# A first cross attention whose preparation is split into pieces of one step each, with every engine's order written out

## The chip, the cores and the metric

One core of one Trainium2 chip runs the whole program. The metric is the device time in microseconds (us) of one execution. Its engines are called by the profile's names: PE (TensorE matmul), PEld (its weight loads), DVE (VectorE), ACT (ScalarE), POOL (GpSimd) and SP (SyncE, which issues most DMAs).

## What is computed

The reference runs eight blocks one after the other on `x` (8 batches x 256 tokens x 128) and a context (8 x 512 x 96). The change is in the first block, a cross attention with 16 heads of 8 elements, and in the seams beside it:

```python
Qp = query @ Wq + bq                      # query = layernorm(x)
K = _l2norm(key @ Wk + bk)                # key = value = the context
V = value @ Wv + bv
Q = _l2norm(Qp)
scores = jnp.einsum('bhqd,bhkd->bhqk', Q, K) * SCALE     # 16 heads of 8
attn = jax.nn.softmax(scores, axis=-1)
out = jnp.einsum('bhqk,bhkd->bhqd', attn, V)
out = out @ Wo + bo
x = out + Qp
return (x - mu) / jnp.sqrt(var + LN_EPS) * ln_gamma + ln_beta
```

The block's result is added to `x`. The second block, a feed-forward network (FFN) with eight experts, begins with two norms of `x`, a router of 8 logits, and a choice of the top two.

## The kernel before

**Tiling.** `x` lies as 16 tiles of 128 tokens. A *group* is four of them, two batches. For every batch b the keys are prepared (context transposed, `turn_ctx`; projected and biased, `biased_k`; the rows' squares and their inverse roots, `row_sizes`; scaled, `scaled_rows`; transposed and cut into three bf16 parts, `pieces`; stored to DRAM as `kd` and read back as `kS`, eight heads of 72 rows). For every even b the queries of its group are prepared alike (`norm_x`, `turn_x`, `project_q`, `pieces`, then `qd` and `qS`). `project_v` makes the values, and `place_values` copies them on POOL into a ring of two tiles `va`, whose columns of ones make a head's sum of exponentials appear as one more row of its product.

**The loop.** A batch has 8 steps, 64 in all: a step does two of four head pairs' scores (`step_probs`: eight score matmuls `sc`, and two ACT exponentials of 128x1024, L617) and, two steps behind, the value products (`step_values`: sixteen `po` records). Four steps make a *half* of a batch, eight heads. `half_sums` then copies `po` to `pv` on ACT (L633). In the next step `half_values` multiplies `pv` by the matrix `moves`, which brings every head's sum to all of its 16 rows, takes the reciprocal of 128x256 (L641) and multiplies (L642). `finish` applies Wo (`pw`), adds the base `qpo`, norms (L654 to 656) and adds to `x_sb` on POOL (L657). `normed_group` (two norms, `z`) and `route_group` (the transposes of `z`, the router's `pl`, softmax and top two) prepare the FFN.

**The order.** `at_step(t, name, f, ...)` enters a piece into `plan`; `beside(t)` runs in step t all that is due, after the scores' matmuls and ahead of the value products. Matmuls and transposes keep the written order. Ahead of the loop all engines do (`in_order`). In the loop the other engines' order is a scheduler's choice, except that nothing in it goes ahead of what is written before the loop (`fenced`), and that pieces given through `queued` keep their own order. A piece has one step: its matmuls, its DVE and POOL operations, and its DMAs are all written there.

**Memory that turns.** `banks("l0x", 2, 2)`: two pairs of PSUM banks for scores, two banks for `po`, and two single banks which all other matmuls (`pt`, `pct`, `pk`, `pq`, `pv`, `pd`, `pw`, `pl`) take in turn (`bank`). `kS` and `qS` have three buffers each, `ct`, `un`, `cut`, `v0` two, `qp`, `kp`, `sq`, `pv0` one.

**SP** issues, in the plan's steps: a batch's context at t0-24, the loads of `kS` and `qS` at t0-8 and t0-4 (t0 = 8b), a group of `x` at 6 and 16, 15 broadcasts of biases (`load_bc`) at 10, rows of biases at 17, and FFN weights at 18, 26 and 42. `spread_rows` builds a matrix for a much later block, in six pieces on POOL at steps 21 to 31 (L160 to L169).

Of the kernel before, what the change touches and what calls it, by code (L numbers as in the profile page):

```python
# [9 lines left out]
F32 = mybir.dt.float32  # L10
# [21 lines left out]
def kernel(ctx: ExitStack, tc: tile.TileContext, a: dict, out: bass.AP):  # L32
# [50 lines left out]

    @contextmanager
    def fenced():

        traced = nc.cur_bb.bb.instructions
        last = traced[-1]
        before = {i.engine: i for i in traced}
        yield  # L90
        start = next(k for k in reversed(range(len(traced))) if traced[k] is last) + 1
        for i in traced[start:]:
            if i.engine in before:
                behind(i, before[i.engine])

    def queued(f, *args):
        with in_order():
            f(*args)
# [227 lines left out]
    def layernorm(src, dst, n):  # L326
# [7 lines left out]
        rsqrt(rstd[:, :n], mv[:, :n, 1], n, LN_EPS, ALU.add)  # L334
        for t in range(n):
            nc.vector.tensor_scalar(
                dst[:, t, :], src[:, t, :], mv[:, t, 0:1], rstd[:, t : t + 1], ALU.subtract, ALU.mult
            )

# [64 lines left out]

    def normed_group(pool, g):
# [3 lines left out]
        layernorm(x_sb[:, gs], xl[:, gs], 4)  # L409
        nc.gpsimd.tensor_tensor(x_sb[:, gs], x_sb[:, gs], xl[:, gs], ALU.add)  # L410
        layernorm(xl[:, gs], z, 4)
# [4 lines left out]
    def route_group(pool, g, z):  # L416

        gs = slice(4 * g, 4 * g + 4)
        transpose4(z, xlT[:, 512 * g : 512 * (g + 1)])
        pl = bank("pl")[:, : 4 * NE].rearrange("p (t e) -> p t e", e=NE)  # L420
# [5 lines left out]
        softmax8(pool, p, 4)  # L426
# [9 lines left out]
    with banks("l0x", 2, 2), tc.tile_pool(name="l0x", bufs=2) as pool, tc.tile_pool(  # L436
# [21 lines left out]
        def norm_x(g):  # L458
            gs = slice(4 * g, 4 * g + 4)
            layernorm(x_sb[:, gs, :], xl[:, gs, :], 4)  # L460
# [4 lines left out]
        def row_sizes(src):  # L465

            sq = pool.tile([P, 4, D], F32, tag="sq", name="sq", bufs=1)
            nc.gpsimd.tensor_tensor(sq, src, src, ALU.mult)
# [11 lines left out]
        def unit_rows(src):  # L480

            return scaled_rows(src, row_sizes(src))

        def pieces(un, name, first=False):

# [12 lines left out]
            else:  # L498
                nc.gpsimd.tensor_copy(cut[:, 1, :], rest)
                nc.gpsimd.tensor_tensor(cut[:, 2, :], rest, cut[:, 1, :], ALU.subtract)  # L500
            if name == "kd":
# [40 lines left out]

        moves = pool.tile([P, P], F32, name="moves", bufs=1)

        def make_moves():
            m, i = (v.rearrange("p (g h o) -> p g h o", g=4, h=2) for v in (moves, ident))
            for h in range(2):
                nc.gpsimd.tensor_copy(m[:, :, h], i[:, :, 1])

# [12 lines left out]
        def output_base(g, qp):  # L562

            gs = slice(4 * g, 4 * g + 4)
            nc.gpsimd.tensor_tensor(qpo[:, gs], qp, over(bc["L0_xattn_bo"], 4), ALU.add)
            nc.gpsimd.tensor_tensor(x_sb[:, gs], x_sb[:, gs], over(bc["L0_xattn_ln_beta"], 4), ALU.add)

        def project_q(g):
            qp = biased_q(g)
            un = unit_rows(qp)  # L570
            output_base(g, qp)
            return un
# [12 lines left out]
        def project_k(b):  # L585
            return unit_rows(biased_k(b))
# [44 lines left out]
        def half_sums(po):  # L631
            pv = pool.tile([P, S], F32, tag="pv0", name="pv0", bufs=1)
            nc.scalar.copy(pv, po)  # L633
            return pv

        def half_values(pv, oT, half):

            pd = bank("pd")[:, :S]
            matmul(pd, lhsT=moves, rhs=pv, start=True, stop=True)
            den = pool.tile([P, S], F32, tag="den0", name="den0")  # L640
            nc.vector.reciprocal(den, pd)  # L641
            nc.vector.tensor_tensor(oT[:, half], pv, den, ALU.mult)  # L642

        def finish(b, oT):
# [10 lines left out]
            layernorm(y, y, 2)  # L655
# [11 lines left out]
        at_step(0, ("kd", 1), pieces, ("un_k", 1), "kd")  # L667
        for b in range(B):
            t0 = 8 * b

            if b >= 2:
                late = t0 - 16 if b == 2 else t0 - 21
                at_step(t0 - 24, ("ct", b), load_ctx, b)
                if b % 2 == 0:
                    at_step(late, ("xl", b), norm_x, b // 2)
                    at_step(late + 2, ("xlT", b), turn_x, b // 2)
                at_step(late + 1, ("turn", b), turn_ctx, b, ("ct", b))
                at_step(late + 1, ("max", b), max_ctx, b)
                if b % 2 == 0:
                    at_step(late + 3, ("un_q", b), project_q, b // 2)  # L680
                at_step(late + 4, ("un_k", b), project_k, b)
                at_step(late + 5, ("v", b), project_v, b)
                if b % 2 == 0:
                    at_step(late + 6, ("qd", b // 2), pieces, ("un_q", b), "qd")
                at_step(late + 7, ("kd", b), pieces, ("un_k", b), "kd")
            for half in range(2):
                if (b, half) != (0, 0):
                    at_step(t0 - 8 + 4 * half, ("kS", b, half), stacked_k, ("kd", b), half)
                    at_step(t0 - 8 + 4 * half, ("qS", b, half), stacked_q, ("qd", b // 2), half, b % 2)
                    at_step(t0 - 2 + 4 * half, ("va", b, half), place_values, b, half, ("v", b))  # L690
            at_step(t0 + 11, ("done", b), lambda b, oT: finish(b, oT), b, ("oT", b))
        for g in range(4):
            at_step(16 * g + 20, ("z", g), normed_group, pool, g)
            at_step(16 * g + 26, ("r", g), route_group, pool, g, ("z", g))
# [3 lines left out]
        at_step(3, ("moves", 0), make_moves)  # L698
# [1201 lines left out]
```

## Time and profile before

| | us |
|---|---|
| runs | 1621.91, 1623.96, 1627.40 |
| median | 1623.96 |
| the profiled execution | 1627.38 |
| its span | 1625.7 |

| group in the loop (33.6 to 258 us) | count | busy us | mean ns |
|---|---|---|---|
| ACT `pT<-sc` 128x1024 (L617) | 128 | 124.3 | 1026 |
| PE `po<-pT,va` (L60) | 1024 | 78.7 | 430 |
| PE `sc<-qS,kS` (L60) | 508 | 77.8 | 298 |
| PE `pd<-pv,moves` (L60) | 30 | 10.2 | 423 |
| POOL `ln_rstd` and `l_inv` 128x4 (L324) | 18 | 18.4 | 1018 |
| POOL spread rows (L160 to L169) | 24 | 16.5 | 688 |
| DVE `rest<-pt,cut` (L494) | 10 | 6.7 | 672 |
| ACT `pv<-po` (L633) | 16 | 6.1 | 380 |

A float32 matmul is two records, a transpose and a bf16 matmul are one. Records of PE overlap a little, so that its busy sum is not its time; the distance between two starts is. In rows of the timeline the columns are start, length, engine, line, operation, tiles, and in brackets the idle time ahead of it with what ended it.

### The profile page before, as it was taken

Reading aid. Unit: us, or ns where it says so; the run is one execution under the profiler, and the core shown is the slowest. Engines: PE = TensorE matmul, PEld = TensorE weight load, DVE = VectorE, ACT = ScalarE, POOL = GpSimd, SP = SyncE. Lnnn points to the kernel's source line nnn. Section 1 sums busy time; section 2 is a strip of 40 time slices with the busy share of each in tenths; the row PEclk is TensorE's granted clock in tenths of the full one; section 3 lists DMA queues with packets and bytes.
Section 4 is the critical chain, followed back from the end, with each engine's and each line's share of the span. In section 5 each row is a group of like instructions: output and inputs, shape, how many; then the busy total and the mean of one; then the engine's idle time right before and its main releaser. Section 6 shows DMA issues by size and latency. Waiting matters only on the chain.

```text
span 1625.7 us, 24905 instructions
## 1 busy us (share of the span) xinstructions
PE 1518.5 (93%) x9038; PEld 900.6 (55%) x9041; DVE 1000.9 (62%) x2444; ACT 819.8 (50%) x1671; POOL 505.9 (31%) x680
## 2 busy tenths in 40 slices
PE   5898798999997898999999999999999999999996
PEld 4555455776464474565555554555555555555554
DVE  5565656786776546667764555666666665656563
ACT  2564575454755655556553222545555545455552
POOL 4456321001222223333440001324243424334342
PEclk9887899999999898999999999999999999999997
DMA  5563330020511113121200000000000000000000
GB/s 124 147 152 85 100 87 27 1 71 14 185 52 53 41 44 97 60 78 54 78 27 1 1 1 1 1 1 7 4 8 4 7 4 11 1 10 6 6 8 13
DMA packets 72519, 67.90 MB, mean 42 GB/s; under 512 B 17059, under 2 KB 61390, under 8 KB 70862
## 3 DMA queue, kind: packets, MB, share of 16 engines
q1 hardware_dynamic: 69518, 63.68, 13.5%
q0 software_dynamic: 1536, 2.11, 0.4%
q8 instruction: 72, 1.18, 0.3%
q10 hardware_dynamic: 1344, 0.52, 0.1%
q14 instruction: 49, 0.40, 0.1%
HBM read 44.80 MB, written 21.50 MB: 41 GB/s over the span
## 4 chain that ended last, share of the span: by engine, by line
PE 75%; DVE 10%; POOL 5%; ACT 5%; issue 3%; DMA 1%; POOLq 0%; SPq 0%; ACTq 0%; DVEq 0%
PE sc L60 14%; PE poh L60 11%; PE tp L63 11%; PE po L60 6%; PE ph L60 4%; PE pkh L60 3%; PE poe L60 3%; PE pqh L60 3%; PE acc L60 3%; PE pox L60 2%; PE pkv L60 2%; PE pvh L60 2%; POOL ln_rstd L324 2%; PE pyw L60 2%; PE pxv L60 2%
## 5 line engine op out<-in xcount | busy, mean ns | idle before, releaser
L1438 POOL TENSOR_SCALAR prob<-prob,at_inv 128x512 f32<-128x512 f32 x384 | 261.7, 695 | 482.9 <-DVE at_inv L1436 375.7
L1451 ACT COPY probT<-tp 128x512 f32<-128x512 f32 x192 | 112.8, 587 | 335.2 <-PE tp L63 333.9
L1431 ACT ACTIVATE prob<-sc,at_neg 128x512 f32<-128x512 f32 x384 | 261.3, 688 | 32.9 <-DVE at_neg L1428 28.4
L1428 DVE TENSOR_REDUCE at_neg<-sc 128x2 f32<-128x1024 f32 x192 | 233.3, 1216 | 65.6 <-PE sc L60 65.3
L63 PEld LDWEIGHTS tp<-ident,prob 128*128 128x128 f32 x1664 | 178.4, 141 | 147.9 <-issue 101.3
L63 PE MATMUL tp<-ident,prob 128*128 128x128 f32 x1664 | 227.1, 279 | 1.5 <-POOL prob L1438 1.4
L60 PE MATMUL sc<-kTh,qT 64*128 64x512 f32 x768 | 217.6, 644 | 0.0
L60 PE MATMUL poh<-probT,vh 128*64 128x256 f32 x1536 | 186.5, 385 | 1.8 <-ACT vh L1402 1.0
L617 ACT ACTIVATE pT<-sc 128x1024 f32<-128x1024 f32 x128 | 124.3, 1026 | 76.1 <-PE sc L60 75.5
L324 POOL TENSOR_TENSOR ln_rstd<-rs_v,mhalf 128x4 f32<-128x4 f32 (+1 forms) x52 | 48.0, 924 | 354.2 <-DVE rs_v L323 342.4
L60 PEld LDWEIGHTS poh<-probT,vh 128*64 128x64 f32 x1536 | 101.9, 136 | 78.1 <-issue 14.1
L1451 DVE COPY probT<-tp 128x512 f32<-128x512 f32 x192 | 130.5, 679 | 1.1 <-PE tp L63 0.9
L60 PEld LDWEIGHTS sc<-kTh,qT 64*128 64x128 f32 x768 | 58.4, 186 | 81.7 <-issue 51.4
L1436 DVE RECIPROCAL at_inv<-at_tot 128x2 f32<-128x2 f32 x192 | 31.6, 164 | 100.7 <-ACT prob L1431 79.5
L60 PE MATMUL sc<-qS,kS 72*128 72x256 bf16 x512 | 78.6, 299 | 4.1 <-DMA qS<-qd 3.5
L1463 DVE COPY oTh<-poh 128x256 f32<-128x256 f32 x96 | 40.7, 424 | 62.3 <-PE poh L60 60.4
L60 PE MATMUL po<-pT,va 128*32 128x256 f32 x1024 | 78.7, 430 | 0.2 <-ACT pT L617 0.2
L1431 ACT ACTIVATION_READ_ACCUMULATOR prob<-sc,at_neg 128x1 f32 x384 | 77.5, 202 | 0.0
L60 PEld LDWEIGHTS <-kS 72*128 72x128 bf16 x512 | 49.0, 106 | 44.4 <-issue 31.5
L943 ACT ACTIVATE hT<-ph,cols 128x512 f32<-128x512 f32 x64 | 43.3, 687 | 52.3 <-PE ph L60 48.9
L60 PE MATMUL pkh<-ctxT,w 96*128 96x512 f32 x128 | 67.0, 605 | 0.0
L60 PE MATMUL pvh<-w,ctxT 96*128 96x512 f32 x128 | 66.4, 600 | 0.0
(386 smaller groups left out, 2417.6 us busy)
## 6 DMA issues: line engine op xcount, KB each, us to landing
kS<-kd SPq DMA_DIRECT2D x48, 192.0 KB
kTh<-kv SPq DMA_DIRECT2D x6, 1024.0 KB
vh<-kv SPq DMA_DIRECT2D x6, 1024.0 KB
kv<-xl SPq DMA_DIRECT2D x20, 256.0 KB
qd<-cut SPq DMA_DIRECT2D x24, 192.0 KB
qS<-qd SPq DMA_DIRECT2D x48, 96.0 KB
kv<-shelf SPq DMA_DIRECT2D x16, 256.0 KB
kd<-cut SPq DMA_DIRECT2D x8, 384.0 KB
```

The costliest lines, as they stand in the source:

```text
L60: return tc.keep_in_program_order(nc.tensor.matmul(*args, **kw))
L63: return tc.keep_in_program_order(nc.tensor.transpose(*args, **kw))
L324: nc.gpsimd.tensor_tensor(dst, v[:, :n], mhalf[:, :n], ALU.pow)
L617: nc.scalar.activation(pT[:, g], sc, AF.Exp, scale=8.0 ** -0.5)
L943: nc.scalar.activation(hT[:, c, :], ph, AF.Gelu, bias=col("L0_ffn_b1", 2 * e + c))
L1428: nc.vector.tensor_reduce(neg, sc, AX.X, ALU.max, negate=True)
L1431: nc.scalar.activation(prob[:, q, h, :], sc[:, h, :], AF.Exp, bias=neg[:, one], scale=1.0, accum_out=tot[:, one])
L1436: nc.vector.reciprocal(inv, tot)
L1438: nc.gpsimd.tensor_scalar(prob[:, q, h, :], prob[:, q, h, :], inv[:, h : h + 1], 1.0, ALU.mult, ALU.mult)
L1451: copy(probT[:, h, :, q * P : (q + 1) * P], tp)
L1463: nc.vector.tensor_copy(oT[:, c, :], po)
```

## The change

- `layernorm` becomes `norm_sizes` (statistics, variance, inverse root) and `norm_rows`; `row_sizes` becomes `row_squares` and `row_inverses`; `pieces` becomes `cut_pieces` and `store_pieces`.
- Longer pieces are generators whose stages `in_stages` puts on a list of steps: queries over six steps, keys over five within six, values of a half over three, `finish` over two, `normed_group` over three, `route_group` over three.
- The whole loop now stands within `in_order`, so that every engine keeps the written order; `fenced` and `queued` go. `beside(t - 1)` runs in pass t, so a piece of plan step t stands one pass later than that number. "Pass t" below is the loop's t.
- `moves` goes. A half's sums are taken from `pv` transposed: two matmuls of `pv` with 8 columns of the identity give 32 sums for each query; their reciprocals are widened on POOL (`wide`, 128x256), transposed by two transposes (`pd`), and multiplied with `pv`.
- Loads of `kS` and `qS` stand at t0-6 and t0-2; `residual_base` is a stage of its own.
- The six `spread_rows` pieces move to the plan of the FFN stage, steps 16 to 26, which isn't within `in_order`.
- `route_group` of group 2 comes nine steps behind its `z`, after the loop's last scores.

```diff
-        def half_sums(po):
+        first_sums = ident.rearrange("p (g h j m) -> p g h j m", g=4, h=2, j=2)[:, :, 1, :, 0]
+        def half_values(po, oT, half):
             pv = pool.tile([P, S], F32, tag="pv0", name="pv0", bufs=1)
             nc.scalar.copy(pv, po)
-            return pv
-        def half_values(pv, oT, half):
+            yield
+            ps = bank("ps")[:, :16].rearrange("p (q g j) -> p q g j", q=2, g=4)
+            for q in range(2):
+                matmul(ps[:, q], lhsT=pv[:, q * P : (q + 1) * P], rhs=first_sums, start=True, stop=True)
+            inv = pool.tile([P, 2, 4, 2, 2], F32, tag="inv0", name="inv0")
+            for h in range(2):
+                nc.vector.reciprocal(inv[:, :, :, h, :], ps)
+            wide = pool.tile([P, 2, P], F32, tag="wide0", name="wide0", bufs=1)
+            nc.gpsimd.tensor_copy(
+                wide.rearrange("p q (i m) -> p (q i) m", m=8),
+                inv.rearrange("p q g h j -> p (q g h j)").unsqueeze(2).to_broadcast([P, 32, 8]),
+            )
+            yield
             pd = bank("pd")[:, :S]
-            matmul(pd, lhsT=moves, rhs=pv, start=True, stop=True)
-            den = pool.tile([P, S], F32, tag="den0", name="den0")
-            nc.vector.reciprocal(den, pd)
-            nc.vector.tensor_tensor(oT[:, half], pv, den, ALU.mult)
+            for q in range(2):
+                transpose(pd[:, q * P : (q + 1) * P], wide[:, q], ident)
+            nc.vector.tensor_tensor(oT[:, half], pv, pd, ALU.mult)
...
+        def unit_pieces(biased, name, n, base=None):
+            p = biased(n)
+            sq = row_squares(p)
+            yield
+            inv = row_inverses(sq)
+            yield
+            un = scaled_rows(p, inv)
+            yield
+            cut = cut_pieces(un)
+            yield
+            got[name, n] = store_pieces(cut, name)
+            if base:
+                output_base(n, p)
+                yield
+                residual_base(n)
...
+        def in_stages(ts, name, f, *args):
+            stages = []
+            def run():
+                if not stages:
+                    stages.append(f(*[got[v] if isinstance(v, tuple) else v for v in args]))
+                try:
+                    next(stages[0])
+                except StopIteration as end:
+                    got[name] = end.value
+            for t in ts:
+                plan.append((t, len(plan), run))
...
+            late = 0 if b == 2 else t0 - 19
             if b >= 2:
-                late = t0 - 16 if b == 2 else t0 - 21
-                at_step(t0 - 24, ("ct", b), load_ctx, b)
+                at_step(late - 1, ("ct", b), load_ctx, b)
                 if b % 2 == 0:
-                    at_step(late, ("xl", b), norm_x, b // 2)
+                    in_stages((late, late + 1), ("xl", b), norm_x, b // 2)
                     at_step(late + 2, ("xlT", b), turn_x, b // 2)
-                at_step(late + 1, ("turn", b), turn_ctx, b, ("ct", b))
+                at_step(late + 3, ("turn", b), turn_ctx, b, ("ct", b))
...
+                    in_stages(
+                        (late + 4, late + 5, late + 6, late + 7, late + 8, late + 9), ("q", b),
+                        unit_pieces, biased_q, "qd", b // 2, True,
+                    )
+                at_step(late + 4, ("max", b), max_ctx, b)
+                in_stages(
+                    (late + 5, late + 6, late + 7, late + 9, late + 10), ("k", b), unit_pieces, biased_k, "kd", b
+                )
+                at_step(late + 8, ("v", b), project_v, b)
...
+                t = t0 + 5 + 4 * half
+                in_stages((t, t + 1, t + 2), ("o", b, half), half_values, ("po", b, half), ("oT", b), half)
+            in_stages((t0 + 12, t0 + 13), ("done", b), finish, b, ("oT", b))
-        for g in range(4):
-            at_step(16 * g + 20, ("z", g), normed_group, pool, g)
-            at_step(16 * g + 26, ("r", g), route_group, pool, g, ("z", g))
+        for g in range(3):
+            t = 16 * g + 22
+            in_stages((t, t + 1, t + 2), ("z", g), normed_group, pool, g)
+            if g == 2:
+                t += 9
+            in_stages((t + 3, t + 4, t + 5), ("r", g), route_group, pool, g, ("z", g))
...
-        fence = fenced()
-        fence.__enter__()
...
+            for t in range(8 * B + 2):
...
+                if t > 0:
+                    beside(t - 1)
...
-        at_step(1, normed_group, pool, 3, to="z")
+        at_step(1, lambda: whole(normed_group(pool, 3)), to="z")
...
+        for r in range(2):
+            for i in range(3):
+                at_step(16 + 6 * r + 2 * i, spread_rows, r, i)
```

## The prediction

> **What bounds the kernel now.** I read the slices of the page first, then the windows by stage, then TensorE's order of time inside the first attention, then the groups of that stage.
>
> ```profile
> PE   5898798999997898999999999999999999999996
> ...
> PEclk9887899999999898999999999999999999999997
> ```
>
> Seen here: slices 0 to 5 (a slice is 40.6 us) are the first cross attention, and there TensorE is neither full nor at full clock. Behind slice 7 both rows stand at 9, so little is to be won there, and nothing there is edited. The windows (columns: PE, PE load, DVE, ACT, POOL busy with counts, granted clock, DMA share, GB/s) cut the attention at its stalls:
>
> ```profile
> 0.00:32.50 32.50, 14.55 (x60) 12.48 (x61) 14.98 (x31) 5.43 (x9) 13.51 (x23) 1.00 0.50 129
> 32.50:57.80 25.30, 22.45 (x153) 14.98 (x154) 12.89 (x31) 12.11 (x13) 10.23 (x13) 0.81 0.58 130
> 57.80:110.40 52.60, 50.26 (x511) 32.63 (x508) 33.09 (x78) 37.08 (x45) 26.13 (x37) 0.93 0.59 148
> 110.40:134.60 24.20, 16.89 (x133) 10.73 (x130) 13.29 (x31) 8.78 (x12) 15.92 (x21) 0.77 0.43 100
> ```
>
> Compare the counts: 511 matmul records in 52.6 us, 133 in 24.2 us. Where nothing waits, TensorE runs at a step of 2 to 2.9 us; from 110.4 on it lost over half. TensorE's order of time shows how:
>
> ```profile
> 110.35 1.05 PE L60 MATMUL sc<-qS,kS 72*128 72x256 bf16 x8
> 114.90 2.07 PE L60 MATMUL pk<-w,ctxT 96*128 96x128 f32 x8 [3.51 <-DVE ctxT L451]
> 116.91 1.94 PE L60 MATMUL po<-pT,va 128*32 128x256 f32 x16
> ...
> 127.79 0.66 PE L63 MATMUL pt<-ident,un 128*128 128x128 f32 x4 [1.87 <-DVE v L596]
> 129.54 0.63 PE L63 MATMUL pt<-ident,z 128*128 128x128 f32 x4 [1.10 <-DVE den L641]
> 130.95 1.87 PE L60 MATMUL pl<-w,xlT 128*128 128x8 f32 x8 [0.78 <-DVE xlT L108]
> 132.76 1.94 PE L60 MATMUL po<-pT,va 128*32 128x256 f32 x16
> ```
>
> A piece of preparation sits in TensorE's queue and its input is late in VectorE's; then the same sixteen value products take 1.94 us and not 1.07 (half clock). So each wait is paid twice. The bound of this stage is TensorE's in-order queue waiting on chains VectorE-GpSimd-VectorE.
>
> **The size of it.** From the first score (32.52) to the first matmul of the FFN (262.93) are 230.4 us. TensorE's own work, from full-clock starts (eight sc 0.98 us, sixteen po 1.00, eight pk, pv, pq, pw or pl 0.89, four pt or pct 0.45 to 0.55, two pd 0.45): 64 x 1.98 = 126.7; 12 pk/pv 10.7; 6 pct 3.3; 16 pt 7.2; 3 pq 2.7; 16 pd 7.2; 8 pw 7.2; 3 pl 2.7; rest 0.2. Sum 167.9, so 62.5 us are lost to waits and clock. That is the most the change can win.
>
> **Part by part.**
>
> *Inverses.* These rows are touched:
>
> ```profile
> L641 DVE RECIPROCAL den<-pd 128x256 f32<-128x256 f32 x15 | 26.3, 1756 | 26.0 <-PE pd L60 26.0
> L601 POOL COPY va<-v 128x256 f32<-128x256 f32 x14 | 5.5, 396 | 21.1 <-PE po L60 21.1
> L565 POOL TENSOR_TENSOR xl<-qp,bc_tile 128x512 f32<-128x512 f32 x3 | 3.8, 1269 | 0.0
> ```
>
> VectorE loses 16 x 1.76 and gets 16 x 2 reciprocals of 16 elements; the nearest row, the reciprocal of 128x4, is 0.18 each. Net -1.4 us a half, -22 in all, off TensorE's path except that work stops queueing behind it. TensorE: pd 0.45 becomes ps (two products, half of a pl: 0.45) and two transposes (half of a pt, 0.22, taken 0.30): +0.30 x 16 = **+4.8 us**, on the path. GpSimd gets `wide`, 128x256, with no row of its own: between 0.40 (the va copy, as many elements) and 1.27 (row L565, twice as many and two inputs); I take 0.5, nearest the copy. The handover ps, reciprocals, `wide`, transpose is 0.1+0.35+0.1+0.5+0.1 = 1.15 us against 1.98 us of po and sc that lie between on TensorE, so it is hidden with 0.8 to spare, and the pieces ahead of it on GpSimd are few in each pass.
>
> *Pieces, one a pass.* For each pass I added the pieces' rows by engine. TensorE is largest in nearly all (2.0 to 3.5 us); over 64 passes TensorE has 170, ScalarE 138, VectorE 112, GpSimd 89 us. VectorE overflows where routing falls (18 small operations of 0.22 and others: 5.4 us in passes 28 and 44), GpSimd where the norm falls (5.0 us in passes 23 and 39). Most handovers now have a pass or two in hand: q from pq to its transposes is 5.0 us of chain against three passes (8 us). The context's load for b=3 went out at 44.61 for transposes that waited for it until 49.52 (2.82 us and more); now it is issued in pass 5 for pass 9, behind few DMAs, and I take that wait as gone. The residual's beta (1.27 us of GpSimd) only changes its place, and a second sq buffer costs nothing. Four remain late:
>
> 1. *z.* Its three stages stand in passes 23, 24, 25, and TensorE's transposes of z in pass 26, ahead of that pass's value products and next scores. Taking 0 at the scores of pass 23: ScalarE's cast ends 3.3, rest 4.0, sizes 5.5; GpSimd has `wide`, va, residual and the cut's two operations first and raises the power by 7.1; rows 8.3, sizes 9.8, power 11.0, rows 12.2, gamma 12.9, GpSimd's beta 14.3 (rows 1.12, 1.53 for four statistics, 1.02, 1.27). TensorE arrives after 2.88+2.28+2.53+0.98 = 8.7. **Wait 5.7 us**, for groups 0 and 1; group 2's transposes are moved by 9 and do not wait.
> 2. *xl* in passes 16 and 32: waits of 1.0 and 1.4 by the same sum.
> 3. *After routing* (passes 28 to 31): v's bank is cleared behind it, the next transposes wait some 2 us; twice, 4.
> 4. *qS at pass 16.* SP has the kd store (pass 11), then the 15 broadcasts, in this trace from 76.15 to 85.73 = 9.6 us, then kS and qS, 2.7 us, landing within 2.7 (88.57 to the use at 91.25). The loads moved two steps later; from pass 11 they land 16.9 us on, and pass 16 starts 14.2 on. 0 to 2.7 of wait, up to 3.5 of half clock; I take 3.
>
> *The clock.* The rule of the Trainium skill (TensorE: Matmul & The Clock Gate, Part 1) is that the array falls to half rate after an idle window of about 3.4 us. By it only the z waits would cost clock. The trace is stricter: after 1.90 us idle at 144.05 the products at 145.81 took 1.94 us, and some 4.7 us were lost until 155. By the rule, the waits listed under 2 to 4 cost their 9.4 us; by the row each that nears 2 us costs up to 4.7 more. But after 1.29 us at 164.53 the next sc took 1.05, so I charge waits under 1.5 us nothing, and 1.6 us after each z wait (as after 181.55: pd 1.19, po 1.94, sc 1.20 where 0.60, 1.07, 1.05 are usual): z costs 2 x 7.3 = 14.6.
>
> *Spread rows* are moved out of this stage (16.5 us of GpSimd). The order list shows them not in the FFN but hoisted to the ramp, all six pieces ahead of or between the ramp's own GpSimd work (a piece is 0.52+1.28+0.75 or 1.16). Two go ahead of sq<-kp: GpSimd was free from 7.3 to 10.8, they take 5.5, so kp's squares start 2.0 later, and kd, qd and the first scores +2.2. The skill (SBUF — State Buffer, section on its two sides) adds that VectorE with two SBUF inputs and GpSimd lock each other out for a whole instruction; the trace agrees (un at 92.52 took 1.52, 0.69 alone, beside sq). By the rows alone +2.2, with that lock +3; **+3.0** taken, bounds 0 and 5.
>
> *End and FFN.* Last po to first ph was 5.0 us; now 0.48+0.45+0.45+1.05+0.3+0.5+0.89, about the same, 2.5 of it waiting. Group 2's routing now lies behind it on VectorE, 20 x 0.22 ahead of the last y, so group 3's norm and its pl come up to 3.7 later: 0 to 3.7, **+2.0**. TensorE's order behind it is the same in both.
>
> **Sum.** Work 167.9+4.8 = 172.7. Losses kept: cold start 4.5 (three steps at half clock, as now), coupling 6 (passes 15 to 23 took 21.98 us for 20.86 of work, 5%, in the loaded two thirds), z 14.6, xl 2.4, routing 4, qS 3, end 2.5 = 37.0. Together 209.7 against 230.4: -20.7; ramp +3.0, FFN +2.0: **-15.7 us**. The profiled run took 1627.38 (its span 1625.7 and 1.7 around it): 1611.7. The median, 1623.96, is 3.4 lower: **1608.3**.
>
> **Rivals.** *More is won (0.10):* the coupling is nil and z's waits fall in passes that are long anyway. For it: VectorE is freed of 22 us. Against: the chain of z is longer than three passes whatever they hold. -15.7-6.0-14.6 = -36.3: 1588. *It is given back (0.13):* pinning makes ScalarE and VectorE stand where the scheduler let other work pass; twice the coupling (+6), qS at its upper bound (+3), waits of 1 to 2 us at the row's clock (+6): about 1623. For it: only two single banks turn for all pieces, three of them in passes 27 and 43. Against: the loads by pass. *Slower (0.15):* `wide` is the new wait. Place: the transposes pd in each of 16 halves; it bites once `wide` lands over 2 us behind ps, and turns the sign when these waits sum to over 16 us. If GpSimd stands 1.8 us behind in its queue, each of 16 halves waits 1.0, and half of them cost 1.6 of clock as well: 1608+16+13 = 1637. For it: GpSimd's 5.0 us in passes 23 and 39. Against: `wide` is first in its pass in nearly all.
>
> **Numbers.** Forecast 0.62 (its own range 1592 to 1619). A difference under 0.3%, 4.9 us, can't be told from none. Faster: 0.62+0.10+0.02 = 0.74; within: 0.08; slower: 0.15+0.03 = 0.18. The range 1590 to 1628 leaves out the most of the first and third rivals.
>
> **What would show it.** Right: records of 400 or more in each 40 us of the attention; waits of about 5 us at `pt<-ident,z` twice; no wait at pd; the first sc near 35.5; first ph near 245. Wrong: pd waiting for `wide` L668 in most halves; a wait at sc for qS of over 5 us; a granted clock still near 0.8 from 60 to 200 us.

## The result, and the profile after

The changed kernel is slower: 1632.27 us median of 20 runs (1624.32 to 1638.55) against 1624.23 of 20 runs of the kernel before (1619.77 to 1627.40), ratio 1.0050 with a 95% interval of 1.0035 to 1.0066. The forecast was 1608.3, a gain. The profiled executions lie above their medians, the changed kernel's (1637.70) by 5.4 us and that of the kernel before (1627.38) by 3.2, so sizes read in one trace are those of one execution.

The two rows of slices after:

```profile
PE   4977898999998798999999999999999999999996
...
PEclk9987888999999898999999999999999999999997
```

They look like those of before; behind slice 7 nothing has changed. The windows, cut again at the stalls (columns as before: PE, PE load, DVE, ACT, POOL busy with counts, granted clock, DMA share, GB/s):

```profile
35.60:85.60 50.00, 48.50 (x430) 31.45 (x430) 23.16 (x58) 32.59 (x38) 23.34 (x34) 1.00 0.46 112
85.60:95.30 9.70, 1.06 (x17) 0.43 (x17) 4.40 (x13) 1.06 (x2) 3.44 (x5) 0.74 0.86 159
95.30:126.20 30.90, 30.80 (x314) 20.80 (x314) 16.44 (x43) 21.85 (x26) 14.17 (x17) 0.92 0.56 146
126.20:133.30 7.10, 0.00 (x0) 0.00 (x0) 5.59 (x17) 1.83 (x3) 3.50 (x3) 0.62 0.63 161
133.30:190.60 57.30, 54.41 (x501) 35.94 (x501) 31.83 (x101) 32.62 (x39) 22.20 (x28) 0.84 0.39 102
190.60:197.60 7.00, 0.00 (x0) 0.00 (x0) 5.47 (x16) 1.84 (x3) 3.50 (x3) 0.65 0.65 168
197.60:269.00 71.40, 66.66 (x670) 42.88 (x670) 28.96 (x109) 43.68 (x52) 17.48 (x26) 0.88 0.27 60
```

The many small losses of before have become three holes: 9.7, 7.1 and 7.0 us in which TensorE does next to nothing. But read the counts of the others too: TensorE is busy for 48.5 of the first 50.0 us with 430 records, and in the third window 314 records fit into 30.9 us. The first runs at a lower pace without standing still, which the busy time does not show. The list of TensorE's waits in the loop (who waits, for whom, us in total, times, the longest) names the holes:

```profile
PE pt L63 <- POOL z L417: 14.2, 2, 7.2
PE sc L60 <- DMA qS<-qd: 12.3, 2, 8.6
PE pt L63 <- DVE v L618: 2.9, 2, 1.9
PE pd L63 <- POOL wide L668: 2.2, 3, 1.1
PE pt L63 <- DVE xl L324: 1.9, 3, 0.9
```

TensorE's order of time around the first wait for `z`:

```profile
125.12 1.05 PE L60 MATMUL sc<-qS,kS 72*128 72x256 bf16 x8
133.34 1.11 PE L63 MATMUL pt<-ident,z 128*128 128x128 f32 x4 [7.17 <-POOL z L417]
134.38 1.94 PE L60 MATMUL po<-pT,va 128*32 128x256 f32 x16
...
146.25 1.94 PE L60 MATMUL po<-pT,va 128*32 128x256 f32 x16
148.12 1.13 PE L60 MATMUL sc<-qS,kS 72*128 72x256 bf16 x8
...
150.07 1.07 PE L60 MATMUL po<-pT,va 128*32 128x256 f32 x16
```

Sixteen value products take 1.94 us where 1.07 is usual, and they still do 12.9 us after the wait is over. From 133.3 to 148.1 there is no gap in which TensorE waits, and half of these 14.8 us is lost: 7.4 us, as much as the wait itself. Behind the second wait it is 12.0 us (197.6 to 209.6), behind the one for `qS` 5 us (95.3 to 100.3), and from the first score on 21.5 us (35.6 to 57.1, about 1 us of it waits).

VectorE's rows of `z` and the GpSimd operation beside them, in the changed kernel, and then VectorE's rows in the kernel before:

```profile
129.17 2.05 DVE L324 TENSOR_SCALAR z<-xl,ln_mv,ln_rstd 128x128 f32<-128x128 f32 x4 [0.53 <-POOL ln_rstd L308]
129.11 1.26 POOL L413 TENSOR_TENSOR x_sb<-x_sb,xl 128x512 f32<-128x512 f32 x1
...
112.41 1.12 DVE L336 TENSOR_SCALAR z<-xl,ln_mv,ln_rstd 128x128 f32<-128x128 f32 x4 [1.13 <-POOL ln_rstd L324]
```

The same four operations take 0.9 us longer beside GpSimd's addition to `x_sb`; before, that addition ran at 109.98 us and was over. The second `z` shows the same (2.04 us). That the one slows the other is read from these times and was not tested by a run.

From first score to first `ph` the loop takes 233.5 us (35.61 to 269.06; before 230.4). With TensorE's work of 172.7 from the prediction, 60.8 are lost: start 10.3 of half speed and 1.0 of waits; pass 16 8.6 + 2.5; `z` 14.2 + 13.4; the short waits for `v`, `xl`, `wide` and `pv` 6.8, with 3.2 of half speed behind them. That is 60.0, so about 1 us is left for everything else.

### The profile page after: what moved, and what is told of

It is laid out like the page before. It is cut to its first block, busy times and chain, and to the rows that moved or that the text cites. A ratio compares the mean times of both kernels' runs of the same rounds, so it can differ in the third digit from the quotient of the medians.

```text
span 1636.0 us, 25066 instructions
## 1 busy us (share of the span) xinstructions
PE 1521.3 (93%) x9105; PEld 906.9 (55%) x9105; DVE 992.7 (61%) x2460; ACT 819.3 (50%) x1671; POOL 512.8 (31%) x694
## 3 DMA queue, kind: packets, MB, share of 16 engines
q1 hardware_dynamic: 69518, 63.68, 13.4%
## 4 chain that ended last, share of the span: by engine, by line
PE 77%; DVE 10%; POOL 4%; ACT 4%; issue 3%; DMA 1%; SPq 0%; POOLq 0%; ACTq 0%; DVEq 0%
PE sc L60 14%; PE poh L60 11%; PE tp L63 11%; PE po L60 5%; PE ph L60 5%; PE pkh L60 3%; PE poe L60 3%; PE pqh L60 3%; PE acc L60 3%; PE pox L60 3%; PE pkv L60 2%; PE pvh L60 2%; POOL ln_rstd L308 2%; PE pyw L60 2%; PE pxv L60 2%
## 5 line engine op out<-in xcount | busy, mean ns | idle before, releaser
L60 PEld LDWEIGHTS poe<-w,hT 128*128 128x128 f32 x512 | 63.5, 199 | 9.6 <-issue 5.0
L60 PE MATMUL poe<-w,hT 128*128 128x128 f32 x512 | 65.9, 284 | 1.8 <-ACT hT L995 1.7
```

Source lines behind the costliest of these rows:

```text
L60: return tc.keep_in_program_order(nc.tensor.matmul(*args, **kw))
```

## The experiments

All time ratios are to the kernel before, run beside each on the same chip. The runs are from several chips, so the medians of two rows should be compared by their ratios. "Profiled" is the time of the execution that was profiled; in it, "loop" is first score to first `ph`, and "FFN" first `ph` to the first `pl` behind it. Where it lies far from the median (e2, e10 and e12 by 6 us above, e8 by 6 below), a loop is that much less typical.

| kernel | median us | ratio, 95% interval | profiled | first score | loop | FFN |
|---|---|---|---|---|---|---|
| before | 1624.23 | 1 | 1627.38 | 32.5 | 230.4 | 19.8 |
| changed | 1632.27 | 1.0050 (1.0035 to 1.0066) | 1637.70 | 35.6 | 233.5 | 24.8 |
| e1 z later | 1614.13 | 0.9934 (0.9916 to 0.9951) | 1615.48 | 35.7 | 209.6 | 24.8 |
| e2 broadcasts later | 1622.35 | 0.9985 (0.9972 to 0.9998) | 1628.35 | 35.8 | 226.8 | 24.8 |
| e5 TensorE kept busy | 1620.78 | 0.9984 (0.9969 to 0.9999) | 1621.34 | 36.1 | 219.5 | 24.8 |
| e4 old inverses | 1629.30 | 1.0036 (1.0024 to 1.0047) | 1631.67 | 36.2 | 228.0 | 24.8 |
| e3 spread rows late | 1630.21 | 1.0055 (1.0035 to 1.0074) | 1632.14 | 32.2 | 236.3 | 24.9 |
| e7 group 2 earlier | 1624.40 | 1.0030 (1.0021 to 1.0040) | 1625.29 | 36.0 | 230.9 | 20.0 |
| e10 xl later | 1621.00 | 1.0006 (0.9991 to 1.0021) | 1627.60 | 35.9 | 226.6 | 24.8 |
| e12 e10, warm start | 1621.08 | 1.0001 (0.9990 to 1.0013) | 1627.22 | 36.0 | 226.1 | 24.8 |
| e8 all moves | 1602.61 | 0.9890 (0.9873 to 0.9908) | 1596.77 | 32.3 | 209.1 | 20.0 |
| e9 e8, old inverses | 1598.04 | 0.9864 (0.9842 to 0.9887) | 1597.74 | 32.5 | 205.6 | 20.0 |
| e11 e9, broadcasts split | 1592.52 | 0.9827 (0.9813 to 0.9840) | 1594.19 | 33.1 | 202.8 | 20.0 |
| e13 e11, warm start | 1595.01 | 0.9835 (0.9820 to 0.9849) | 1595.01 | 31.7 | 204.1 | 20.0 |
| e14 e11, new inverses | 1601.58 | 0.9883 (0.9867 to 0.9899) | 1602.98 | 32.2 | 212.0 | 20.0 |
| e15 before, new inverses | 1629.94 | 1.0049 (1.0031 to 1.0067) | 1633.70 | 34.1 | 239.5 | 19.8 |

The theory was that the waits for `z` and `qS` took the gain and that each is paid twice. Its rivals: that half speed comes whatever waits there are, that something else is late in any case, and that the inverses cost what the plan wins.

### The waits for z (e1)

```diff
             if g == 2:
                 t += 9
+            else:
+                t += 3
             in_stages((t + 3, t + 4, t + 5), ("r", g), route_group, pool, g, ("z", g))
```

> The routing stages of groups 0 and 1 stand three passes later (28, 29, 30 and 44, 45, 46 instead of 25, 26, 27 and 41, 42, 43); nothing else is moved. Theory (each wait at z is paid twice, once standing and once at half speed behind it): the waits of 7.2 and 7.0 us at the transposes of z go, and with them about 7 and 6 us of half speed; the loop from the first score to the first ph gets 20 to 28 us shorter than the changed kernel's 233.5, the time is about 1608. Rival A (the half speed comes by itself, whatever the waits): only the 14 us of standing go, the time is about 1618. Rival B (something queued behind z is late anyway, so that the wait only changes its place): less than 7 us, time about 1627 or above.

The loop fell by 23.9 us, from 233.5 to 209.6, and the time from 1.0050 to 0.9934, 1.2% or 19 us. The theory's 20 to 28 holds for the loop of the profiled executions. The 19 us by the ratios lie between it and the 14 us of rival A; what decides against A is that the products behind `z` now run at full speed. Rival B falls. TensorE's order of time at the same place in e1:

```profile
129.60 1.05 PE L60 MATMUL sc<-qS,kS 72*128 72x256 bf16 x8
132.52 0.44 PE L63 MATMUL pd<-ident,wide 128*128 128x128 f32 x2 [1.87 <-POOL wide L668]
132.88 1.93 PE L60 MATMUL po<-pT,va 128*32 128x256 f32 x16
...
137.24 0.60 PE L63 MATMUL pt<-ident,z 128*128 128x128 f32 x4
137.77 1.07 PE L60 MATMUL po<-pT,va 128*32 128x256 f32 x16
```

The transposes of `z` no longer wait, and something smaller is late next: `wide`, 1.87 us, because GpSimd has the norm's operations ahead of it (126.94 to 132.06 us). It too is paid for with half speed, 3.5 us of it.

### Is it the idleness? (e5)

```diff
+    def busy_pe(n):
+        pt = bank("pt")
+        for i in range(n):
+            transpose(pt[:, i % 4 * P : (i % 4 + 1) * P], ident, ident)
...
     def route_group(pool, g, z):
+        if g < 2:
+            busy_pe(40)
         transpose4(z, xlT[:, 512 * g : 512 * (g + 1)])
```

> TensorE gets transposes of the identity, which nobody reads, to do while it would wait: 16, 6 and 13 of them at its three waits ahead of the first scores, 50 ahead of the scores of pass 16, 40 ahead of the transposes of z of groups 0 and 1. All waits stay, only TensorE doesn't stand idle in them. Theory (the half speed behind a wait is caused by the idleness): the products behind pass 16 and behind z run at full speed at once (sixteen po near 1.07 us and not 1.94), and the cold start from the first score on shrinks from 21 us at half speed to under 6; the time falls by 12 to 22 us to about 1610 to 1620, with the waits still there. Rival (half speed is decided by something else than TensorE's idleness, such as the clock granted by the throttle, or the busy transposes do not count): no gain, 0 to +6 us for the added work.

In e5, around the first `z`:

```profile
122.81 4.53 PE L63 MATMUL pt<-ident 128*128 128x128 f32 x40
130.14 0.66 PE L63 MATMUL pt<-ident,z 128*128 128x128 f32 x4 [2.80 <-POOL z L417]
130.73 1.07 PE L60 MATMUL po<-pT,va 128*32 128x256 f32 x16
```

`z` is as late as ever, 7.3 us behind the last useful product. But the value products take 1.07 us at once. The same holds behind the wait in pass 16; behind the second `z` some half speed stayed (one group of products at 191.0). The loop fell by 13.9 us with the data as late as before (in pass 16 by 1.2 us less), close to the 15.9 lost to half speed there by the trace of the changed kernel (7.4 + 6.0 + 2.5). The time fell by 0.66% or 11 us, just short of the 12 to 22 expected. So some 40% of what these three waits cost together (22.8 us of standing, 15.9 of half speed) was half speed, and idleness brings it. At the cold start e5 missed: half speed ended at 43 us, came back behind waits of 1.33 and 0.86 us for `xl`, and went on to 57.

### The wait for qS (e2)

```diff
-        at_step(10, ("bc", 0), load_bc, nc.sync, 6, len(bc_from))
+        at_step(15, ("bc", 0), load_bc, nc.sync, 6, len(bc_from))
```

> The fifteen broadcasts on SP's queue are issued in step 15 instead of step 10, behind the loads of kS and qS for pass 16. Theory (these broadcasts hold SP's queue, and the q load of pass 16 stands behind them): the wait of 8.6 us before the scores of pass 16 falls under 1 us and about 2.7 us of half speed go with it; 8 to 11 us shorter than the changed kernel, about 1622. Rival (the pieces of k are stored late, and the broadcasts only fill the time): the wait stays at 5 us or more, gain under 4 us. Third way: the broadcasts now hold back the loads for pass 20, and a wait of 3 to 9 us appears there; gain about nothing.

SP's queue in the changed kernel shows what stood ahead (start, time to issue, and how many DMAs):

```profile
75.81 0.43 SPq L174 DMA_DIRECT2D bc_tile<-in_L_ffn_ln_g_dram  x1
...
83.89 0.43 SPq L174 DMA_DIRECT2D bc_tile<-in_L_ffn_br_dram  x1
84.42 3.11 SPq L545 DMA_DIRECT2D kS<-kd  x3
89.32 1.33 SPq L537 DMA_DIRECT2D qS<-qd  x3
```

With the broadcasts moved, the wait of 8.64 us is gone and so is 0.65% of the time, 11 us; pass 20 has no wait, and the first one behind the broadcasts is 0.51 us at pass 24. The loop of the profiled execution, the longest of its 14 runs, fell by 6.7 only: the pass now meets the late `xl` (waits of 0.23 and 0.91 us) that the longer wait had covered, with 3.4 us of half speed behind. Without the broadcasts ahead of them, `kS` took 1.18 us to issue and `qS` followed 1.2 us after it began, so the broadcasts cost more than their own 8.5 us of issue.

### The xl waits and the cold start (e10, e12)

```diff
-                    at_step(late + 2, ("xlT", b), turn_x, b // 2)
+                    at_step(late + 3, ("xlT", b), turn_x, b // 2)
```

> Only the transposes of xl stand one pass later (passes 3, 19, 35 instead of 2, 18, 34). Theory (two waits of 0.7 to 1.4 us close to each other, at the transposes of xl, throw TensorE back to half speed before the cold start is over): no wait at xl and no half speed from 48 to 57 us, so 5 us less there, 1 to 3 us less at each of the other two places; 5 to 9 us under the changed kernel, about 1624 to 1627. Rival (the cold start lasts until about 57 whatever stands at xl): the products still take 1.9 us until 55 to 57; gain of 1 to 3 us.

0.44%, 7 us, for waits that sum to 1.9 us. In the changed kernel a wait of 0.62 for `wide` and two of 0.23 and 0.91 for `xl`, all within 2.9 us, threw TensorE back (its order of time, the last of the four transposes):

```profile
161.81 0.37 PE L63 MATMUL pt<-ident,xl 128*128 128x128 f32 x1 [0.91 <-DVE xl L324]
162.11 1.94 PE L60 MATMUL po<-pT,va 128*32 128x256 f32 x16
```

In e10 the wait of 0.62 stays, now one pass ahead of `xl`; the transposes come without a wait, and the same products run at full speed:

```profile
158.57 0.60 PE L63 MATMUL pt<-ident,xl 128*128 128x128 f32 x4
...
159.54 1.07 PE L60 MATMUL po<-pT,va 128*32 128x256 f32 x16
```

At the start, half speed ended at 49.7 us and not at 57.1. So some 7 of the 21.5 us came from `xl`, and about 14 from the start itself, in this execution. e12 adds the unread transposes at the start (16, 6 and 45):

> As the last one, and TensorE gets 16, 6 and 45 transposes of the identity that nobody reads at its three waits ahead of the first scores, so that it is busy nearly up to them. Theory (the cold start is only idleness in the ramp): the first eight scores take near 1.0 us and not 1.87, as do the next; the 10 us of half speed from the first score on go, half of them is time: 4 to 6 us under the last one. Rival (half speed at the start of the loop comes from elsewhere): the same time as the last one, or 1 us more.

TensorE's order of time in e12, from the first score on:

```profile
36.04 1.03 PE L60 MATMUL sc<-qS,kS 72*128 72x256 bf16 x8 [0.84 <-DMA qS<-qd]
37.75 0.60 PE L60 MATMUL sc<-qS,kS 72*128 72x256 bf16 x4 [0.67 <-ACT pT L644]
38.66 0.65 PE L60 MATMUL sc<-qS,kS 72*128 72x256 bf16 x4 [0.32 <-ACT pT L644]
...
41.80 1.94 PE L60 MATMUL po<-pT,va 128*32 128x256 f32 x16
```

The first scores run at full speed, and that is where the gain ends: ScalarE's exponentials (1.03 us each, for four scores of 0.5) cannot follow before there are value products to put between, TensorE waits 0.67 and 0.32 us for them, and is at half speed from 39.1 to 49. The time is that of e10. My theory missed that the first passes are ScalarE's. Why half speed then lasts 10 us under work without a gap stays open.

### Spread rows and group 2 (e3, e7)

```diff
-        for r in range(2):
-            for i in range(3):
-                at_step(16 + 6 * r + 2 * i, spread_rows, r, i)
...
+        for r in range(2):
+            for i in range(3):
+                at_step(49 + 6 * r + 2 * i, ("later", 1 + 3 * r + i), spread_rows, r, i)
```

> The six spread pieces stand in the loop's plan in passes 49 to 59 and no longer in the ramp; the rest is the changed kernel. Theory (they hold up GpSimd in the ramp): the first score comes at 32.5 and not 35.6, the loop keeps its 233.5 us with both z waits and the wait for qS; time 3 us under the changed kernel, about 1629. Rival (GpSimd's 16 us are then missing in the loop): the copies `wide` wait behind a piece and TensorE with them, three times or more for over 1 us each with half speed behind; gain 0 or a loss of up to 6.

The first score came 3.4 us earlier, and the loop gave back 2.8: one `pd` waited 5.41 us for `wide`. The time is that of the changed kernel (1.0055). The rival's mechanism is right, with one long wait rather than three short ones.

```diff
-                t += 9
+                t += 3
```

> Only the routing stages of group 2 move, from passes 66, 67, 68 (three passes from the loop's end) to 60, 61, 62. Theory (its twenty small operations stand ahead of the last y on VectorE): the stretch from the first ph of the FFN to its first pl falls from 24.8 us to about 20, as before the change; 4 to 5 us less, about 1628, with both z waits, the qS wait and their half speed unchanged. Rival (the FFN's start is bounded by something else, such as group 3's own norm): the stretch stays over 23 and the gain is under 1.5 us.

VectorE at the FFN's start in the changed kernel:

```profile
270.17 0.15 DVE L307 TENSOR_SCALAR rs_v<-ln_mv 128x2 f32<-128x2 f32 x1
270.23 0.18 DVE L437 TENSOR_REDUCE sm_s<-pr 128x4 f32<-128x32 f32 x1
...
274.43 0.19 DVE L447 TENSOR_TENSOR pr<-pr,den 128x32 f32<-128x32 f32 x1
274.54 0.59 DVE L324 TENSOR_SCALAR y<-y,ln_mv,ln_rstd 128x128 f32<-128x128 f32 x2
```

And the same `y` in e7:

```profile
268.03 0.15 DVE L307 TENSOR_SCALAR rs_v<-ln_mv 128x2 f32<-128x2 f32 x1
269.01 0.60 DVE L324 TENSOR_SCALAR y<-y,ln_mv,ln_rstd 128x128 f32<-128x128 f32 x2 [0.83 <-POOL ln_rstd L308]
```

The last `y` stands behind 4.3 us of routing and begins 4.4 us after its variance (`rs_v`), in e7 1.0 us after it: 3.4 us later. With the routing earlier the stretch is 20.0 us and not 24.8, close to the 19.8 before the change. So this is its cause. The time fell from 1.0050 to 1.0030, intervals that overlap; the stretch in the trace is the firmer number.

### All together, and the inverses (e4, e8, e9, e11, e13)

e4 puts the old `moves`, `pd` and 128x256 reciprocal into the changed plan:

```diff
-            ps = bank("ps")[:, :16].rearrange("p (q g j) -> p q g j", q=2, g=4)
...
+            pd = bank("pd")[:, :S]
+            matmul(pd, lhsT=moves, rhs=pv, start=True, stop=True)
+            den = pool.tile([P, S], F32, tag="den0", name="den0", bufs=1)
+            nc.vector.reciprocal(den, pd)
+            yield
+            nc.vector.tensor_tensor(oT[:, half], pv, den, ALU.mult)
```

> The changed kernel's plan with the inverses as they were before: one product with moves and a reciprocal of 128x256 per half on VectorE, in the slots of the new stages (one of the three stages is then empty). Theory (the new inverses are sound, the waits elsewhere took the gain): VectorE gets 22 us more work in the loop, in passes where its chain to z is already late, so the two z waits grow by 1 to 2 us each and others appear: 4 to 15 us slower than the changed kernel, 1636 to 1647. Rival (the new inverses, with two more products and the copy on GpSimd, cost what the plan wins): TensorE gets 4.8 us less, and the time falls by 3 us or more under the changed kernel's.

The loop is 5.5 us shorter, though VectorE has 22 us more to do; the two `z` waits did not grow (6.9 and 6.8). The theory's expectation fell. The intervals of the times overlap, so the sign was open here. e8 has all moves (routing of all three groups at `t += 3`, broadcasts, spread rows, `xl`), e9 the old inverses as well:

> All moves together: the routing stages three passes later for groups 0 and 1 and six earlier for group 2, broadcasts in step 15, spread pieces in passes 49 to 59, and the transposes of xl one pass later. Theory: the parts add up, as they lie in different places: z 18 (measured alone), broadcasts 7 to 10 (measured 6.5 in the loop), spread 3, group 2 4.5, xl 2 to 5: 35 to 40 us under the changed kernel, about 1592 to 1597, 1.7 to 2.0 per cent under the kernel before. Rival (what one move frees is lost again at the next thing that is late, `wide` and xl above all): under 28 us, 1604 or more.

> As the last one, with the inverses as before the change (one product with moves and a reciprocal of 128x256 per half). Theory (TensorE bounds the loop once the waits are gone, and the new inverses give it 4.8 us more to do): 3 to 5 us under the last one. Rival (VectorE, with 22 us more to do, becomes late at xl, pk or pt once the passes are short): 5 to 15 us over the last one, with new waits of over 1 us for VectorE.

The single moves sum to 2.4% (1.16 + 0.65 + 0.44 + 0.20 - 0.05), e8 brought 1.6%: they do not add up, as the rival had it (26 us, where the theory had 35 to 40). GpSimd and then TensorE in e8 show one place where it goes:

```profile
215.60 1.27 POOL L417 TENSOR_TENSOR z<-z,bc_tile 128x512 f32<-128x512 f32 x1 [0.64 <-DVE z L416]
...
217.39 1.28 POOL L146 TENSOR_SCALAR_AFFINE_SELECT sp<-sp 48x512 f32<-48x512 f32 x2
218.75 1.15 POOL L153 TENSOR_TENSOR spread<-spread,sp 48x512 bf16<-48x512 bf16 x1
219.85 0.39 POOL L668 COPY wide<-inv 128x256 f32<-128x256 f32 x1
```

And TensorE's order of time in e8, at that moment:

```profile
220.30 0.69 PE L63 MATMUL pd<-ident,wide 128*128 128x128 f32 x2 [5.39 <-POOL wide L668]
220.92 1.94 PE L60 MATMUL po<-pT,va 128*32 128x256 f32 x16
```

`wide` stands behind `z` and the spread pieces in GpSimd's queue, and TensorE behind `wide`. e9 has no such handover through GpSimd, and is 4.6 us faster by the medians, though the intervals meet. Left in e9 was a wait of 4.09 us for `qS`, behind the broadcasts: the third way of e2 after all, once the passes are short. It stands at pass 24, counted in the trace; "pass 20" in the expectations for e2 and e11 is a miscount. TensorE in e9 at that place:

```profile
106.25 1.86 PE L60 MATMUL sc<-qS,kS 72*128 72x256 bf16 x8 [4.09 <-DMA qS<-qd]
```

e11 issues the broadcasts five at a time:

```diff
-        at_step(15, ("bc", 0), load_bc, nc.sync, 6, len(bc_from))
+        at_step(12, ("bc", 0), load_bc, nc.sync, 6, 11)
+        at_step(15, ("bc", 1), load_bc, nc.sync, 11, 16)
+        at_step(18, ("bc", 2), load_bc, nc.sync, 16, len(bc_from))
```

> All moves with the inverses as before, and the fifteen broadcasts issued five at a time in steps 12, 15 and 18. Theory (the one block of fifteen in step 15 held back the loads of q for pass 20, which waited 4.1 us there): that wait falls under 1 us, and the half speed behind it goes; 4 to 6 us under the kernel with one block (1598), about 1593. Rival (that load is late for another reason, such as the store of q itself): the wait stays at 3 us or more and the time is 1597 or above.

> As the last one, with the busy transposes of the start (16, 6, 45). Theory: 4 to 6 us under the last one, about 1588, 2.2 per cent under the kernel before. Rival: no gain beside the last one.

e11 is the fastest kernel, 1.7% under the kernel before (0.9827), and its interval lies under that of e9. The long wait is gone (0.28 us at pass 24), with 1.57 us left at pass 28. The warm start brought nothing beside it (e13).

### The inverses alone (e14, e15)

e14 is e11 with the changed kernel's inverses; e15 is the kernel before with only these, where the two transposes, the output projection and the routing of a group stand one pass later.

> The fastest kernel so far (all moves, split broadcasts; 1592.5) with the changed kernel's inverses on 32 columns in place of the old ones. Theory (TensorE bounds this loop, and the new inverses give it about 0.3 us more to do in each of 16 halves and make it wait for `wide` where GpSimd is behind): 4 to 10 us slower, 1597 to 1602, with waits at pd for `wide`. Rival (VectorE's 22 us less are worth more where nothing else is late): same or up to 5 us faster.

> The kernel before, with its own plan, and only the inverses on 32 columns: sums, reciprocals and `wide` stand where the old product and reciprocal stood, the two transposes and the product with pv one pass later, and with them the output projection, the norm and the routing of each group. Theory (the inverses by themselves bring nothing, TensorE gets 4.8 us more): 0 to 6 us slower than the kernel before. Rival (VectorE's chains are what is late in this plan, so 1.4 us less of them in each half shorten its waits at pct, pk and pd): 5 to 12 us faster.

Both say the same. In the plan of e11 they cost 9 us (0.9827 to 0.9883, intervals apart); in the old plan, with the pieces behind them one pass later, 8 us (1.0049). The loop got 9.2 and 9.1 us longer. By the prediction's estimate 4.8 us of that is TensorE's own added work, which leaves some 4 for waits. In e14 TensorE waits 10.1 us for `wide`, and two of these waits, of 1.19 and 5.40, stand behind spread pieces, which were put into the loop to free the start; e14 without them there was not run. In e15 the longest wait is this one:

```profile
117.22 0.69 PE L63 MATMUL pd<-ident,wide 128*128 128x128 f32 x2 [8.39 <-POOL wide L640]
```

VectorE and GpSimd ahead of it:

```profile
114.95 0.34 DVE L638 RECIPROCAL inv<-ps 128x16 f32<-128x16 f32 x2
116.77 0.40 POOL L640 COPY wide<-inv 128x256 f32<-128x256 f32 x1
```

The small reciprocals themselves come only at 114.95, behind the norms on VectorE, and `wide` another 1.5 us later, behind a spread piece and `va`. GpSimd is the smaller part of this wait; near this place the kernel before waited 3.51 us too (at 114.90).

## The prediction, step by step

**Where the bound lies:** right. TensorE's in-order queue waits for chains over VectorE and GpSimd (at pass 16 for a load on SP's queue), the long waits are paid twice, and nothing outside this attention and the FFN's start has moved.

**The step that failed** is the price of the waits that it foresaw. It named all four places (`z`, `xl`, the passes behind routing, `qS`); for `z` and `qS` above all, the wait and the half speed behind it were both put too low.

- *z:* "1.6 us after each z wait (as after 181.55)". Of the rows of before I took the cheapest, though 144.05 stood beside it with 4.7 us lost after a wait of only 1.90. Measured: 7.4 and 6.0. The wait itself was put at 5.7 and is 7.17 and 7.04: VectorE's rows of `z` took 2.05 us instead of 1.12, beside GpSimd's addition to `x_sb`, and the first variance (`rs_v`) 1.09 and 0.73 instead of 0.17, beside its `cut`. The sum had both at their length without GpSimd beside them, though the prediction names such a lock for the start. Together 27.6 us where 14.6 were charged; e1 returned 23.9 of the loop.
- *qS at pass 16:* 3 charged, its upper bound 6.2; 8.64 of wait and 2.5 of half speed came. Behind the broadcasts the load of `kS` took 3.11 us to issue and `qS` followed only 4.9 us after it began, its issue ending at 90.65: 6.2 us where the sum had 2.7 for both. The scores began another 4.65 us later, where it had 2.7 to land.
- *cold start:* 4.5 charged "as now"; 10.3 of half speed came. Some 3.5 of the excess came from `xl` (7 us at half speed), whose waits were charged only in passes 16 and 32. The rest stays open.
- *waits under 1.5 us cost nothing:* right for single ones (1.00 us at 156.33 and 1.07 at 252.68 brought no half speed), wrong for several together: 0.62, 0.23 and 0.91 within 2.9 us brought 3.4 us of it.
- *FFN:* +2.0 charged, bounds 0 to 3.7; +5.0 came. The last `y` is 3.4 us later, within the bounds; what they left out is further on, where TensorE waits 1.67 us at its first `poe` (none in e7) and 3.39 for `xlT` (2.41 in e7).
- *coupling:* 6 charged, and 2.5 for the end; for both about 1 is left. Between the waits, passes run at TensorE's own work. The split into pieces does what it was to do.
- *ramp:* +3.0 charged, 3.1 measured, first score at 35.6 as forecast.
- *inverses:* VectorE's 22 us less were called off the path, which is right, but the handover of `wide` was called hidden. In the changed kernel it nearly is (2.2 us in three waits); where `wide` meets other GpSimd work (e8, e14), or the reciprocals are late on VectorE (e15), it is not.

In sum, against a loop of 209.7 us came 233.5. The misses are 13.0 for `z`, 8.1 for pass 16, 6.8 for the start with its waits and 3.6 for the short waits, less 7.7 for coupling and end (which is the remainder). Together 23.8.

**The rivals.** The one on the slow side, `wide` as the new wait in most halves, did not happen: it bit in 3 of 16 halves. The kernel was slower by another mechanism. "Given back" (1623) named `qS` at its bound and waits of 1 to 2 us at half speed, which is the right direction, but added nothing for `z` and the FFN. The signs listed did their work: "a wait at sc for qS of over 5 us" was one of those that would prove the forecast wrong; records per 40 us were 344, 406, 350 and 375 in the four long windows (from their counts), three of them under the 400 named. The third sign nearly came, a granted clock of 0.85 from 60 to 200 us.

**Which part cost.** The move to pieces by pass is sound: with `z`, `xl`, the broadcasts, the spread pieces and group 2 placed with regard to their chains, and with the old inverses, it gives 1.7% over the kernel before (e11). The inverses on 32 columns cost 8 to 9 us in the two plans where they were added alone: they save an engine that has room, give TensorE more to do, and lengthen the path by a handover through VectorE and GpSimd. How much of this the spread pieces in the loop add in e14 is not shown, and a plan with the pieces and a shorter handover was not tried.

## What to carry to other kernels

When every engine's order is pinned, each piece whose chain is longer than the passes given to it becomes a full stop for the queue in front; count the chain of every hand-over with the slowest observed duration, and leave it room beyond that (here one pass more was enough for `xl` and three for `z`). A wait of TensorE costs its length and, in this trace, from nothing (single waits of about 1 us) to as much again (7 us) at half speed; among several recoveries in a trace, do not charge the shortest. Here even the longest of the kernel before, 4.7 us, fell short of the 7.4 and 6.0 that came. Do not free an engine with room by adding a handover to the path.

## What the hardware showed

**Half speed lasts very differently.** With TensorE busy without a gap, the products stayed at half speed for 5, 14.8, 3.4, 12.0 and 3.2 us after waits of 8.6, 7.2, 0.9 (with two shorter ones just ahead), 7.0 and 1.9 us in one execution, so that neither the length of the wait nor that of the work behind it tells how long. The Trainium skill (TensorE: Matmul & The Clock Gate, Part 1) has the array fall to half rate after an idle window of about 3.4 us and come back after a busy one of as much. By that, and this is an estimate from the page, a wait longer than a window costs about 1.7 us to half speed, and a shorter one nothing. The trace differs: waits of 0.62, 0.23 and 0.91 us within 2.9 us were enough to bring half speed, and after 7.17 us it lasted through 14.8 us of unbroken work. Nor does the same wait always do the same: 1.93 us for `v` at 220.26 brought half speed, and in e5 1.90 us at 147.13 and at 208.52 brought none. What decides this, no run here shows.

**The granted clock does not show it.** The window from 35.6 to 85.6 us has a granted clock of 1.00, although TensorE ran at half speed for 21.5 of its 50 us; the lowest values, 0.62 and 0.65, stand in the two windows where it had no matmul at all. In this kernel the length of a known group (sixteen `po`: 1.07 or 1.94 us) is the clock to read.

**Runs spread more.** The changed kernel's 20 runs lie within 14.2 us, the 20 of the kernel before within 7.6. e11 lies within 4.1 us, but that is of 5 runs only, and e8 and e9, with 5 and 6 runs, lie within 9.7 and 11.4. Half speed of varying length behind the same waits would explain the wider spread; it was not measured run by run.
